# A graph network on one core: overflow one-hots sooner, their products later, 512-byte edge fetches, a third PSUM bank for building

## The chip, the core and the metric

The kernel runs on one core of a Trainium2 chip. The metric is the device time of one execution in microseconds (us), the slowest core's time, which here is the only core's. The engines are named as in the profile: PE is TensorE's matrix product, PEld its weight load, DVE is VectorE, ACT is ScalarE, POOL is GpSimd, SP is SyncE, which issues most plain DMAs. Line numbers (L1108) are those of the kernel before.

## What is computed

There are 6250 nodes with 256 features each and 100000 directed edges, sorted by their destination. The input is normalised per row and passed through ReLU; then come four layers that add to each node the sum over its incoming edges and run a small network of three weight matrices; the input is added at the end.

```python
def agg(h):
    return jax.ops.segment_sum(h[src], dst, num_segments=N)
for l in range(NL - 1):
    h = x + agg(x)
    h = jax.nn.relu(h @ W1s[l] + b1s[l])
    h = jax.nn.relu(h @ W2s[l] + b2s[l])
    x = h @ W3s[l] + b3s[l]
h = x + agg(x)
h = jax.nn.relu(h @ cW1 + cb1)
h = jax.nn.relu(h @ cW2 + cb2)
return h @ cW3 + cb3
...
h = jnp.maximum(_layernorm(x, axis=-1), 0.0)
x = x + _L0_gnn_ref(h, src, dst, ...)
```

## The kernel before

**Two ways to sum over edges.** The nodes lie in 49 blocks of 128. Since the sum over edges is linear, the first matrix of a layer is applied ahead of it: `XY` holds z = x W1, split into a high and a low part that TensorE multiplies without loss. Eight *panels* of up to four blocks are summed by TensorE: for each panel the kernel has a matrix of counts (how many edges lead from node s to node d), and `product` (L1545) multiplies it with XY, tile after tile; the product itself stands at L1566, and `prepare` casts the count tiles from bytes to floats ahead of it (L1539 on ScalarE, L1541 on VectorE) into a short ring of tiles. Twenty-one further blocks (17 in the later layers) are *gathered* by GpSimd: each node has K = 17 slots, each slot one row of z fetched from a table in DRAM by its edge's source (L1391), and VectorE adds the rows up (`pair`, L1417 and L1419, then `fold`, L1429 to L1437).

**Overflow.** A node with over 17 edges has the rest of them put into OV = 2 extra slots that its whole block shares: 256 places for a block. `overflow` (L855) finds for each place its edge and its node: it makes a one-hot `hit` on VectorE (L858), multiplies it on TensorE with `taken` into a PSUM bank of its own, `pt` (L861), turns the result into an edge number and a node number `rel` (L868 to L871), and GpSimd fetches the edge's source with `ask` (L607), 4 bytes for each partition. The rows of these two slots arrive in tiles named `last`. At the end of a block's fold VectorE makes a one-hot `hot` of `rel` (L1439), and `add` multiplies it with the rows into the bank `sums` (L1445); `finish` adds the sums to the fold's result (L1455) and hands it to the small network (L1466, L1260, L1289, L1286).

**Stages.** In the start and the edge search, up to 128 us, the kernel finds where each node's edges begin and computes z. The 21 fetches of the first 17 edges' sources, 68 bytes for each partition, are all asked for at its end (L607, tile `idx`), from the input `src` itself. Then comes the *pre-stage*, 36 ticks of two building steps each, 128 to 185 us. A *building step* (`build`, L1086) makes two pieces of a count matrix: VectorE compares cells with lanes into one-hots `lo` and `hi` (L1067; ScalarE copies the pairs for them at L1062), TensorE multiplies them into a bank `bp` (L1108), and ScalarE (L1116) or VectorE (L1118) copies the counts to bytes; L1121 adds each node's own row. Layer 0 follows, 185 to 840 us: seven panels of 49 units, each unit one step of the product, with the rest of building spread among the units. Layers 1 to 3 take the remaining 1560 us and have no building.

**What sets the order.** It is written out by hand. `tick` counts units; `later(n, f)` runs f n units on; `job` gives a span of units in which the small network may run. A `Gathered` object for each layer spreads its work over a clock of planned TensorE time: `passed` adds an instruction's planned time and sends the row gathers that are due (`flow`), each behind a TensorE instruction (`after`), and `advance` runs the events (pair, fold, add) whose slot has come. A block has SLOT = 19 slots; before the change fold stands at slot 16 and add at slot 18. `begin` starts that clock in the pre-stage, at building step READY = 50 for layer 0, with `slot_rows` (L850), which turns all 21 blocks' fetched sources into rows in two VectorE operations (L852, L853): slots that a node does not use get a row of zeros. Overflow of a block runs two blocks ahead.

**Space in PSUM.** There are eight banks: one for `pt`, one for `sums`, two for the small network, two for `agg` of a panel, two for building.

## Time and profile before

| | us |
|---|---|
| median of 3 runs | 2399.58 |
| lowest and highest run | 2398.6, 2402.63 |
| profiled execution, own time | 2401.84 |
| profiled execution, span from first to last instruction | 2400.0 |

The mean granted TensorE clock of the profiled execution is 0.945 of full speed. A row of the groups reads: line, engine, operation, written tile <- read tiles, shapes, number of instructions | busy us, mean ns of one | idle us of the engine just before them and what ended it. "issue" stands for idle time in which the engine waited for nothing that the profile shows, "remote" for a signal that the profile cannot place. A row of the windows gives, for a stretch of the span, its length and then each engine's busy time with the number of instructions, the granted clock, the share of time in which DMA engines were busy, and the GB/s that they moved. A row of the timeline gives start, duration, engine, line, operation and, in brackets, the idle time before it and what ended it.

### The profile page before, as it was taken

The numbers are of one execution on the slowest core, as the hardware profiler recorded it, in microseconds if no ns is written. First come the engines' busy times: TensorE is split into PE (matmuls) and PEld (weight loads), VectorE is DVE, ScalarE is ACT, GpSimd is POOL, SyncE is SP. The second block draws the span as 40 slices with busy tenths as digits, with TensorE's granted clock in tenths as the row PEclk, the third lists the DMA queues.
The fourth block names the chain that finished last, engine by engine and source line by source line (L and its number), as shares of the span: only waits on it lengthen the run. The fifth ranks groups of instructions, "written<-read, shape, count | busy, mean of one in ns | idle before, by whom it ended". The sixth has DMA issues, their size and how long they took to land.

```text
span 2400.0 us, 28926 instructions
## 1 busy us (share of the span) xinstructions
PE 2107.7 (88%) x9071; PEld 1578.9 (66%) x9071; DVE 1242.1 (52%) x2785; ACT 962.7 (40%) x1925; POOL 1515.7 (63%) x1495
## 2 busy tenths in 40 slices
PE   5858788787888899999999899989998998999898
PEld 3635565555555577777777777767776776676665
DVE  6867665655566634444344544443445444544444
ACT  4756555555455643233223342322323422232222
POOL 3346677666776627776677357776777276777773
PEclk9958999898999999999999999999999999999999
DMA  5425545544454645445455465454546454555553
GB/s 174 133 85 161 167 149 163 163 149 143 147 168 152 210 146 169 145 140 169 138 163 164 151 191 153 138 168 136 171 138 194 150 180 141 175 161 181 162 180 94
DMA packets 198743, 375.68 MB, mean 157 GB/s; under 512 B 34210, under 2 KB 125474, under 8 KB 198580
## 3 DMA queue, kind: packets, MB, share of 16 engines
q0 software_dynamic: 69024, 182.29, 25.8%
q1 hardware_dynamic: 127630, 189.61, 24.4%
q10 hardware_dynamic: 1926, 1.85, 0.3%
q8 instruction: 73, 1.20, 0.2%
q14 instruction: 90, 0.74, 0.1%
HBM read 313.88 MB, written 59.39 MB: 156 GB/s over the span
## 4 chain that ended last, share of the span: by engine, by line
PE 80%; issue 7%; DVE 5%; ACT 3%; another core or an unknown queue 3%; DMA 1%; POOL 0%; ACTq 0%; DVEq 0%; POOLq 0%
PE agg L1566 57%; PE ps L1260 6%; PE ps L1289 5%; PE bp L1108 4%; PE sums L1445 3%; ACT at L1116 1%; PE ps L1286 1%; ACT a L1539 1%; PE bp L953 1%; PE ps L1466 1%; DVE acc L1419 1%; PE ps L582 1%; DVE hi L1067 0%; DVE lo L1067 0%
## 5 line engine op out<-in xcount | busy, mean ns | idle before, releaser
L1566 PE MATMUL agg<-a,XY 128*128 128x512 f32 x6076 | 1584.7, 413 | 58.1 <-issue 34.9
L1391 POOL DMA_INDIRECT rows<-table,idx x1152 | 1179.3, 1024 | 631.0 <-PE agg L1566 245.2
L1566 PEld LDWEIGHTS agg<-a,XY 128*128 128x128 f32 x6076 | 1157.2, 195 | 340.4 <-issue 68.8
L1539 ACT CAST a<-at 128x512 fp32r<-128x512 uint8 x943 | 565.0, 623 | 797.8 <-PE agg L1566 574.2
L1541 DVE CAST a<-at 128x512 fp32r<-128x512 uint8 x576 | 257.1, 452 | 534.7 <-PE agg L1566 368.9
L1116 ACT CAST at<-bp 128x392 uint8<-128x392 f32 x402 | 184.2, 488 | 296.7 <-PE bp L1108 107.3
L1419 DVE TENSOR_TENSOR acc<-acc,rows 128x512 f32<-128x512 f32 x432 | 295.6, 684 | 2.7 <-DMA rows<-table,idx 0.4
L1108 PE MATMUL bp<-hi,lo 128*128 128x196 bf16 x1024 | 158.1, 272 | 119.1 <-issue 68.7
L1108 PEld LDWEIGHTS <-lo 128*128 128x128 bf16 x1024 | 87.3, 104 | 207.6 <-issue 154.8
L1391 POOL DMA_INDIRECT last<-table,over x144 | 154.2, 1071 | 67.4 <-PE agg L1566 27.8
L1260 PE MATMUL ps<-h,w 128*128 128x512 f32 (+2 forms) x364 | 159.3, 578 | 7.0 <-issue 7.0
L1067 DVE TENSOR_TENSOR lo<-lanes,pairs 128x512 bf16<-128x512 bf16 x256 | 107.2, 419 | 73.1 <-remote 32.1
L1067 DVE TENSOR_TENSOR hi<-cols,pairs 128x784 bf16<-128x784 bf16 x256 | 142.8, 558 | 0.0
L1289 PE MATMUL ps<-w,h 128*128 128x256 f32 x588 | 135.9, 383 | 3.5 <-ACT h L1473 1.8
L1289 PEld LDWEIGHTS ps<-w,h 128*128 128x128 f32 x588 | 112.5, 192 | 21.8 <-ACT h L1473 2.6
L1118 DVE CAST at<-bp 128x392 uint8<-128x392 f32 x110 | 62.0, 564 | 121.9 <-PE bp L1108 53.2
L1260 PEld LDWEIGHTS ps<-h,w 128*128 128x128 f32 (+1 forms) x364 | 64.8, 186 | 75.2 <-issue 69.3
L1307 DVE TENSOR_TENSOR zz<-ps,w 128x512 f32<-128x512 f32 (+1 forms) x75 | 49.8, 677 | 122.7 <-PE ps L1289 55.9
L1445 PE MATMUL sums<-last,hot 128*128 128x256 f32 x288 | 81.5, 407 | 35.7 <-DVE hot L1439 20.7
L1455 DVE TENSOR_TENSOR u<-u,sums 128x256 f32<-128x256 f32 x72 | 30.0, 417 | 139.9 <-PE agg L1566 112.7
L1445 PEld LDWEIGHTS sums<-last,hot 128*128 128x128 f32 x288 | 54.9, 198 | 63.3 <-DVE hot L1439 25.3
L1391 POOL DMA_INDIRECT last<-table,idx x72 | 75.0, 1041 | 33.5 <-issue 13.7
(167 smaller groups left out, 1080.8 us busy)
## 6 DMA issues: line engine op xcount, KB each, us to landing
at<-mat SPq DMA_DIRECT2D x214, 448.0 KB
mat<-at SPq DMA_DIRECT2D x32, 784.0 KB
rows<-table,idx POOLq DMA_INDIRECT x1152
table<-zz SPq DMA_DIRECT2D x72, 256.0 KB
back<-table SPq DMA_DIRECT2D x120, 128.0 KB
xs<-in_x_dram SPq DMA_DIRECT2D x8, 768.0 KB
table<-zs SPq DMA_DIRECT2D x24, 256.0 KB
out_dram<-zz SPq DMA_DIRECT2D x24, 256.0 KB
```

The source lines that it names most:

```text
L1067: nc.vector.tensor_tensor(o.rearrange("p q (n t) -> p q n t", t=2), values.rearrange("p (n t) -> p n t", t=2)[:, None, :, :].to_broadcast( ...
L1108: mm = nc.tensor.matmul(bp[:, m * HW:(m + 1) * HW], lo[:, q + m, :], hi[:, q + m, :], start=True, stop=True)
L1116: nc.scalar.copy(o, v)
L1118: nc.vector.tensor_copy(o, v)
L1260: mm = nc.tensor.matmul(ps[:mp, :w], weights[l][0][:, c, i * P:i * P + mp], h1[:, c, :w], start=(c == 0), stop=(c == KC - 1))
L1289: mm = nc.tensor.matmul(o, h2[0][:, c, nodes], w3[:, c, :], start=(c == 0), stop=(c == KC - 1))
L1391: got = nc.gpsimd.indirect_dma_start(out=t, out_offset=None, in_=tables[self.l][:, :], in_offset=bass.IndirectOffsetOnAxis(ap=at, axis=0),)
L1419: nc.vector.tensor_tensor(self.acc, self.acc, t, OP.add)
L1445: mm = nc.tensor.matmul(sums[:, :C], self.hot[:, j, :], self.rows.pop((g, K + j)), start=(j == 0), stop=(j == OV - 1))
L1539: nc.scalar.copy(o, mat[l, p][j])
L1541: nc.vector.tensor_copy(o, mat[l, p][j])
L1566: mm = nc.tensor.matmul(agg[c][:, :w], XY[:, j, o:o + P], a[:, :w], start=(j == 0 and half == 0), stop=(j == NT - 1 and half == 1))
```

## The change

- **One bank for masks and sums.** `sums` is allocated once; its first half takes the overflow products, its second half the mask products that went to `pt`.
- **Building gets a third bank**, from two.
- **Edge fetches 512 bytes wide.** Two DMAs at the start, on ScalarE's queue, copy src into a DRAM tile `srcs`, with 128 elements more at its end. The fetches read 128 elements for each partition from it in place of 17 or 1. The first 17 edges' sources are no longer asked for all at once: `slot_rows` runs once for a block, in each of ticks 1 to 21 of the pre-stage, into a tile from the pool of the row gathers, and five ticks later two small VectorE operations (`turn`) write that block's part of `idx`. An overflow's two fetches go into `run` tiles, of which there are two, and six units later `keep` copies the first element of each to `over`.
- **READY** goes from 50 to 54, that is from tick 25 to tick 27, and with it the two first overflows and the start of the row gathers.
- **Events.** The one-hot `hot` becomes an event of its own (`spots`) at slot 8 of its block, from the end of the fold; `add` moves from slot 18 to slot 21, three slots into the next block, but for the last block. Events are sorted by slot.

```diff
     ps_g = ctx.enter_context(tc.tile_pool(name="ps_g", bufs=1, space=PSUM))
+    sums = ps_g.tile([P, 2 * C], F32, name="sums")
     ps_m = ctx.enter_context(tc.tile_pool(name="ps_m", bufs=2, space=PSUM))
...
     from_i = over[:, 0, :]
+    srcs = dram.tile([E + P], I32, name="srcs")
     taken = const.tile([P, NG, 2], BF16, name="taken")
...
     def look(pool):
+        nc.scalar.dma_start(out=srcs[:E].rearrange("(p e) -> p e", p=P - 28),
+                            in_=src.rearrange("(p e) -> p e", p=P - 28))
+        nc.scalar.dma_start(out=srcs[E:].rearrange("(o e) -> o e", o=1),
+                            in_=src[:P].rearrange("(o e) -> o e", o=1))
         firsts_i = pool.tile([1, EB], I32, name="near_i", bufs=1)
...
         at0 = pool.tile([P, NG], F32, name="at0", bufs=1)
-        nc.vector.tensor_scalar(at0, st, float(E - K), None, op0=OP.min)
+        nc.vector.tensor_scalar(at0, st, float(E), None, op0=OP.min)
         nc.vector.tensor_copy(from_i, at0)
-        for c in range(NG):
-            asks.append((idx[:, c, :], src, from_i[:, c:c + 1]))
-        ask(len(asks))
         nc.vector.memset(taken[:, :, 0], 1.0)
...
 
-    def slot_rows():
-
-        nc.vector.scalar_tensor_tensor(live, idx, pad[:, 1:2], live, op0=OP.add, op1=OP.mult)
-        nc.vector.tensor_scalar(idx, live, pad[:, 0:1], None, op0=OP.add)
+    def slot_rows(gath, c):
+
+        t = gath.tile([P, 2, C], F32, name="rows", bufs=7)[:, 0, :P].bitcast(I32)
+        asks.append((t, srcs, from_i[:, c:c + 1]))
+        ask(1)
+
+        def turn():
+            w = live[:, c, :]
+            nc.vector.scalar_tensor_tensor(w, t[:, :K], pad[:, 1:2], w, op0=OP.add, op1=OP.mult)
+            nc.vector.tensor_scalar(idx[:, c, :], w, pad[:, 0:1], None, op0=OP.add)
+
+        later(5, turn)
 
...
         nc.vector.tensor_scalar(hit, slots, gained[:, c:c + 1], None, op0=OP.is_ge)
-        ps = ps_g.tile([P, W], F32, name="pt")
+        ps = sums[:, C:]
         for j in range(OV):
...
         def gather():
+            ts = [hots.tile([P, P], I32, name="run", bufs=2) for _ in range(OV)]
             for j in range(OV):
-                asks.append((over[:, j, c:c + 1], src, e_i[:, j:j + 1]))
+                asks.append((ts[j], srcs, e_i[:, j:j + 1]))
             ask(OV)
+
+            def keep():
+                for j in range(OV):
+                    nc.vector.tensor_copy(over[:, j, c:c + 1], ts[j][:, 0:1])
+
+            later(6, keep)
 
...
                 self.alone = {b + i for b, n, i, _ in self.blocks}
-                self.rows, self.us, self.acc, self.hot = {}, [], None, None
+                self.rows, self.us, self.acc, self.hot = {}, [], None, {}
                 self.order = [(g, k) for g in range(len(self.blocks)) for k in range(SLOT)]
...
                 for g in range(len(self.blocks)):
+                    behind = 3 if g < len(self.blocks) - 1 else 0
+                    self.events.append((SLOT * g + 8, lambda g=g: self.spots(g), False))
                     for k in range(3, K - 1, 2):
-                        self.events.append((SLOT * g + k, lambda g=g, k=k: self.pair(g, k)))
-                    self.events.append((SLOT * g + K - 1, lambda g=g: self.fold(g)))
-                    self.events.append((SLOT * g + SLOT - 1, lambda g=g: self.add(g)))
+                        self.events.append((SLOT * g + k, lambda g=g, k=k: self.pair(g, k), False))
+                    self.events.append((SLOT * g + K - 1, lambda g=g: self.fold(g), False))
+                    self.events.append((SLOT * g + SLOT - 1 + behind, lambda g=g: self.add(g), True))
+                self.events.sort(key=lambda o: o[0])
                 self.n = len(self.events)
...
             def meets(self):
-                return self.due() and self.events[self.done][0] % SLOT == SLOT - 1
+                return self.due() and self.events[self.done][2]
 
...
                 while self.due():
-                    at, run = self.events[self.done]
+                    at, run, _ = self.events[self.done]
                     self.send(at + 1)
...
                     nc.vector.tensor_tensor(self.acc, self.acc, t, OP.add)
+
+            def spots(self, g):
+                c = self.blocks[g][3]
+                hot = self.hot[g] = work.tile([P, OV, P], F32, name="hot", bufs=2)
+                nc.vector.tensor_tensor(hot, colf[:, None, :].to_broadcast([P, OV, P]),
+                                        rel[:, c, :, None].to_broadcast([P, OV, P]), OP.is_equal)
 
...
                 nc.vector.tensor_tensor(u, u, self.rows.pop((g, K - 1)), OP.add)
-                self.hot = work.tile([P, OV, P], F32, name="hot", bufs=2)
-                nc.vector.tensor_tensor(self.hot, colf[:, None, :].to_broadcast([P, OV, P]),
-                                        rel[:, c, :, None].to_broadcast([P, OV, P]), OP.is_equal)
-
             def add(self, g):
                 b, n, i, _ = self.blocks[g]
+                hot = self.hot.pop(g)
                 for j in range(OV):
-                    mm = nc.tensor.matmul(sums[:, :C], self.hot[:, j, :], self.rows.pop((g, K + j)),
+                    mm = nc.tensor.matmul(sums[:, :C], hot[:, j, :], self.rows.pop((g, K + j)),
                                           start=(j == 0), stop=(j == OV - 1))
...
             (l, p, j) for l in range(NLAYER + 1) for p in range(last[l] + 1) for j in range(NT)]
-        sums = ps_g.tile([P, W], F32, name="sums")
         TAIL = 10.0
...
             name="ps_a", bufs=2, space=PSUM
-        ) as ps_a, tc.tile_pool(name="ps_b", bufs=2, space=PSUM) as ps_b:
+        ) as ps_a, tc.tile_pool(name="ps_b", bufs=3, space=PSUM) as ps_b:
             begun = {0: clock[0]}
-            READY = 50
+            READY = 54
             spread = {u: [] for u in range(2, 2 * PRE + 1, 2)}
...
                 if built[0] == READY:
-                    slot_rows()
                     layers[0].begin()
+                if built[0] % 2 == 0 and built[0] // 2 <= NG:
+                    slot_rows(gath, built[0] // 2 - 1)
                 for c in spread[built[0]]:
```

## Prediction

> **What bounds the kernel now.** I read the page first: busy shares, the chain that ended last, the granted clock.
>
> ```profile
> PE 2107.7 (88%) x9071; PEld 1578.9 (66%) x9071; DVE 1242.1 (52%) x2785; ACT 962.7 (40%) x1925; POOL 1515.7 (63%) x1495
> PE 80%; issue 7%; DVE 5%; ACT 3%; another core or an unknown queue 3%; DMA 1%; POOL 0%; ACTq 0%; DVEq 0%; POOLq 0%
> PEclk9958999898999999999999999999999999999999
> ```
>
> TensorE sets the end: 88% busy, 80% of the chain. The change removes none of its large products, so it can only win back TensorE's idle time, or clock. One slice, the third, has a clock of 0.5. So I cut the span at the stages: start, edge search (45 to 128 us, left out), pre-stage of 36 ticks (128 to 185), layer 0 with building beside it (185 to 840), layers 1 to 3.
>
> ```profile
> core 0: us, PE busy (x) PEld busy (x) DVE busy (x) ACT busy (x) POOL busy (x), PEclk, DMA share, GB/s
> 0.00:45.00 45.00, 20.57 (x66) 13.68 (x67) 31.69 (x80) 19.09 (x39) 12.65 (x35) 0.96 0.57 172
> ...
> 128.00:185.00 57.00, 31.70 (x150) 16.38 (x150) 36.19 (x91) 33.48 (x83) 23.54 (x24) 0.52 0.31 96
> 185.00:840.00 655.00, 539.75 (x2617) 386.70 (x2618) 416.01 (x962) 363.81 (x796) 448.80 (x433) 0.93 0.52 161
> 840.00:2400.00 1560.00, 1448.32 (x5860) 1108.34 (x5859) 695.47 (x1471) 490.38 (x892) 994.93 (x969) 0.96 0.51 158
> ```
>
> TensorE is idle for 25 us of the pre-stage, 115 of layer 0 and 112 of layers 1 to 3. TensorE's groups, stage by stage, say ahead of which line:
>
> ```profile
> L1108 PE MATMUL bp<-hi,lo 128*128 128x196 bf16 x144 | 31.4, 346 | 26.4 <-issue 12.4 <-ACT at L1116 5.3 <-DMA idx<-in_src_dram,over 4.5
> ...
> L1108 PE MATMUL bp<-hi,lo 128*128 128x196 bf16 x880 | 126.7, 260 | 92.7 <-issue 56.3 <-ACT at L1116 21.4 <-DVE at L1118 5.8
> ...
> L861 PE MATMUL pt<-taken,hit 128*128 128x2 bf16 x38 | 4.0, 173 | 10.7 <-DVE hit L858 6.1 <-DVE at L1121 3.3 <-issue 1.2
> ...
> L1566 PE MATMUL agg<-a,XY 128*128 128x512 f32 x4740 | 1185.4, 407 | 51.8 <-issue 32.0 <-DVE a L1541 8.4 <-ACT a L1539 8.2
> ...
> L1445 PE MATMUL sums<-last,hot 128*128 128x256 f32 x206 | 59.3, 413 | 29.8 <-DVE hot L1439 15.0 <-issue 5.5 <-DVE u L1436 5.3
> ```
>
> The first row is the pre-stage, the next two layer 0, the last two layers 1 to 3. In layer 0 the idle time stands ahead of building (92.7 of 115), which has two banks. In the later layers L1445, the overflow product, has 29.8 us ahead of it, mostly ended by the fold's own VectorE operations.
>
> **Start (+1).** Two copies of src into DRAM are new on ScalarE's queue. The chain of the start waits for this fetch among others:
>
> ```profile
> 0.74 6.44 DMA near_i<-in_dst_dram
> ```
>
> 400 KB read and 400 KB written at the 172 GB/s of this stretch are 4.7 us of DMA. Nothing waits for the copy itself before 128 us, so the ends are 0 (other fetches hide it: DMA share 0.57) and +4.7 (all of it ahead of near_i). I take +1, near the first.
>
> **Pre-stage, gathers (-2.1).** Before, 21 edge fetches are issued back to back and run into the first ticks:
>
> ```profile
> 127.09 0.96 POOL L607 DMA_INDIRECT idx<-in_src_dram,over  x1 [0.30 <-issue]
> 128.35 0.96 POOL L607 DMA_INDIRECT idx<-in_src_dram,over  x1 [0.30 <-issue]
> ...
> 130.00:150.00 20.00, 6.42 (x30) 3.17 (x28) 5.87 (x14) 6.26 (x14) 13.67 (x14) 0.51 0.16 40
> 152.00:170.00 18.00, 13.27 (x64) 6.86 (x62) 15.19 (x39) 14.36 (x36) 0.00 (x0) 0.50 0.27 89
> ...
> 139.37 0.48 PE L1108 MATMUL bp<-hi,lo 128*128 128x196 bf16 x2 [1.65 <-issue]
> ...
> 157.09 0.88 PE L1108 MATMUL bp<-hi,lo 128*128 128x196 bf16 x4 [0.18 <-ACT at L1116]
> ```
>
> With GpSimd gathering (14 in 20 us) TensorE does 30 matmuls; without, 64 in 18 us, 0.281 us each. Thirty at that pace are 8.4 us, so 11.6 us are lost, 0.83 for each gather. The row at 139.37 shows how: a pair of matmuls waits 1.65 us where clean pairs wait 0.18, though no engine is the bound. After the change one gather is asked for in each of ticks 1 to 21, with TensorE's last matmul ahead of it, and each is 512 bytes wide. Ends: nothing each (-11.6), or 0.83 each as now (17.4, so +5.8). A lone gather meets one of a tick's two hand-offs, so I take half, 0.45 each: 9.5 against 11.6.
>
> The Trainium skill, "SBUF — State Buffer", section "Who interferes with whom", has GpSimd share ports with VectorE alone: "PE and ACT never wait on anyone." By it a gather would cost TensorE nothing, and this term would be -11.6. The two windows above disagree, since both engines halve their pace, though not by which path.
>
> **Pre-stage, VectorE (+3.8).** Two operations on 357 columns go; 42 on 17 columns come, two a tick, with four small copies for the runs.
>
> ```profile
> L852 DVE SCALAR_TENSOR_TENSOR live<-idx,pad,live 128x357 f32<-128x357 int32 x1 | 0.6, 586 | 0.0
> L853 DVE TENSOR_SCALAR idx<-live,pad 128x357 int32<-128x357 f32 x1 | 0.4, 408 | 0.0
> L868 DVE COPY rel<-pt 128x2 f32<-128x2 f32 x21 | 3.2, 154 | 13.1 <-PE pt L861 7.9 <-issue 3.0 <-PE bp L1108 1.5
> L869 DVE SCALAR_TENSOR_TENSOR e_f<-pt,nodes,line 128x2 f32<-128x2 f32 x21 | 4.4, 208 | 0.0
> L871 DVE TENSOR_SCALAR e_i<-e_f 128x2 int32<-128x2 f32 x21 | 3.9, 184 | 0.7
> ...
> 175.53 0.42 DVE L1067 TENSOR_TENSOR lo<-lanes,pairs 128x512 bf16<-128x512 bf16 x1 [0.16 <-PE bp L1108]
> ```
>
> By L869 and L871 two are 0.39 us; the wide L852 and L853 give 0.99 as the upper end. VectorE has 0.16 us of slack in a clean tick (last row), so 0.23 x 21 = 4.8 stands on the path, less 1.0 for the wide ones. Ends: -1 (the gathers' waits cover all) and 0.83 x 21 - 1 = +16.4.
>
> **Pre-stage, third bank (-1.8).** Clean ticks show 0.18 us of TensorE waiting for ScalarE's copy. A third bank keeps ScalarE fed; I take 0.12 in the 15 ticks without a gather. Ends: 0 and 36 x 0.18 = 6.5.
>
> **Pre-stage, the runs (+2.5).** An overflow's fetches go to `run` tiles, two buffers, freed by `keep`, six ticks after. The second overflow's fetches therefore wait on GpSimd for the first one's keep; layer 0's row gathers are queued behind. Its own keep, on VectorE one tick on, waits for those fetches to land, and the one-hots behind it, so TensorE too. Two gathers at 1.26 us (the rows at 127.09 and 128.35) are 2.5; ends 0 and 4. Pre-stage in all: -2.1 + 3.8 - 1.8 + 2.5 = +2.4.
>
> **Layer 0 (-21).** A third bank lets TensorE run one copy further ahead:
>
> ```profile
> L1116 ACT CAST at<-bp 128x392 uint8<-128x392 f32 x402 | 184.2, 488 | 296.7 <-PE bp L1108 107.3 <-remote 90.0 <-PE agg L1566 51.0
> ```
>
> That is 0.49 us more slack ahead of each of 440 steps. The gaps that a copy ended (21.4 + 5.8 = 27.2) are the bank's own price; I take three quarters, 20. Of the 56.3 "issue", where nothing is seen to be late, I take none, since a long stall empties any number of banks; its end is all of it. L861 keeps its wait for hit, a hot one-hot half a block sooner takes 3 off L1445, and row gathers, begun two ticks later, run 2 us denser: -20 - 3 + 2. Masks now share the sums' bank, so a mask might wait for L1455's read; in the order of instructions no such wait is new, hence 0. Ends 0 and -84. What is late next is ScalarE's cast of the adjacency tile, for the product behind the building step.
>
> **Layers 1 to 3 (-19).** All waits ahead of the overflow product, then one of them in time:
>
> ```profile
> PE sums L1445 <- DVE hot L1439: 15.0, 4, 6.7
> ...
> PE sums L1445 <- issue: 5.5, 1, 5.5
> PE sums L1445 <- DVE u L1436: 5.3, 2, 3.5
> PE sums L1445 <- DVE u L1437: 4.0, 2, 3.2
> ...
> 1679.17 0.42 DVE L1541 CAST a<-at 128x512 fp32r<-128x512 uint8 x1
> 1679.51 0.42 DVE L1429 TENSOR_TENSOR u<-XY 128x256 f32<-128x256 f32 x1
> ...
> 1681.22 0.42 DVE L1439 TENSOR_TENSOR hot<-colf,rel 128x256 f32<-128x256 f32 x1
> ...
> 1681.69 1.65 PE L1445 MATMUL sums<-last,hot 128*128 128x256 f32 x3 [5.50 <-issue]
> ```
>
> Nine gaps. VectorE, held up till 1678, runs the cast of the next tile (done at 1679.59), then the fold and the one-hot (1681.64), and TensorE starts at 1681.69. With the one-hot made half a block earlier and the product three gathers later, TensorE goes on once the cast is there: 2.1 us of the 5.5. What held VectorE up stays. Nine times 2.1 is 19. Ends: 0 (the next tile's cast is as late) and -29.8. The fold has the same length as before, less the one-hot, and finish still follows. Clock 0.96 leaves at most 4% of 1560 us, of which I count none.
>
> **Sum.** +1 + 2.4 - 21 - 19 = -36.6. The profiled execution took 2401.84 us (span 2400.0), the three runs 2398.6 to 2402.63 with median 2399.58; it lies among them, so 2401.84 - 36.6 = **2365 us**.
>
> **Rivals.**
>
> *Narrow fetches are the trouble (2327, chance 0.22).* One rule would make the widening the main gain: narrow fetches disturb what follows.
>
> ```profile
> L607 POOL DMA_INDIRECT idx<-in_src_dram,over x21: 951/955/1322, 120.3 to 146.3; - x21
> ...
> L607 POOL DMA_INDIRECT over<-in_src_dram,e_i x42: 951/957/1301, 171.9 to 762.4; - x42
> ...
> 415.52 0.95 POOL L607 DMA_INDIRECT over<-in_src_dram,e_i  x1 [0.30 <-issue]
> ...
> 425.43 0.87 PE L1108 MATMUL bp<-hi,lo 128*128 128x196 bf16 x4 [7.65 <-issue]
> ```
>
> For it: layer 0's longest gap (7.65 us) opens two microseconds after a 4-byte fetch. Against it: GpSimd's time is the same at 68 and 4 bytes a partition, and the gap at 1676 comes among 1 KB row gathers alone. It would take another 9.5 off the pre-stage and half of the 56.3 "issue": 2365 - 9.5 - 28 = 2327. The Trainium skill, "DMA: Bandwidth & Descriptors", section "Specifications", gives 512 B as the least transfer for line rate, with a read-modify-write below.
>
> *The waits only move (2397, chance 0.11).* TensorE's gaps end with the tile for L1566 in place of a bank or a one-hot. For it: 8.2 and 8.4 us ahead of L1566 end with those casts already. Then the two stages give 8 together, against +3.4: 2397.
>
> *Gathers set the pre-stage's pace (2411, chance 0.15).* If a gather makes its tick as slow as in the window from 130 (7.5 ticks in 20 us, 2.67 each), 21 such ticks, 15 of 1.125 (16 ticks in 18 us) and the wait of 2.5 make 75.5 us where 57 stood: +18.5, and +1 at the start. It ends slower once the later stages give less than 19.5; where late hand-offs, and not buffers, make the gaps, a bank and an earlier one-hot give some 10: 2401.84 + 9.5 = 2411. Against it: each fetch stands alone among a tick's work.
>
> **How the numbers follow.** The forecast (2345 to 2390) gets 0.52. A measurement here can tell 0.2%, that is 2394.8 to 2404.4 for no change. Faster: 0.52 + 0.22 + 0.04 of the moved waits = 0.78; same: 0.07; slower: 0.15. The range, 2325 to 2403, holds the forecast, most of the first rival and the second.
>
> **What would show it.** Right: the pre-stage at 57 to 62 us with matmul pairs waiting under 1 us; the idle time ahead of L1108's line near 70 in layer 0, with a copy's share below 10; ahead of the overflow product under 12 in layers 1 to 3, and L1566's idle time not up by the same. Wrong: a pre-stage over 70 us; "issue" ahead of building below 30 (narrow fetches); L1566's idle time in the later layers over 70 (moved). The most doubtful term is layer 0's.

## The result and the profile after

The changed kernel takes 2416.52 us (median of 6 runs, 2410.72 to 2423.85); the kernel before takes 2401.09 beside it (6 runs, 2391.3 to 2403.4). The ratio is 1.0069, with a 95% interval of 1.0047 to 1.0091: **slower by 0.7%**, some 16 us, where 1.5% faster was forecast. The profiled execution of the changed kernel took 2423.85 us, 22 more than that of before.

The page of the changed kernel, busy times and the granted clock:

```profile
span 2422.0 us, 28894 instructions
...
PE 2120.1 (88%) x9071; PEld 1577.8 (65%) x9071; DVE 1245.0 (51%) x2867; ACT 961.0 (40%) x1925; POOL 1516.9 (63%) x1495
...
PEclk9958998899998999999999999999999999999888
```

TensorE is as busy as before (2107.7 then, the same 9071 products), in a longer span. Where the 22 us lie is read from six instructions that mark the stages, in the timeline of the kernel before: the first building product, the first product of layer 0, and the last activation of each layer's last panel.

```profile
129.79 0.50 PE L1108 MATMUL bp<-hi,lo 128*128 128x196 bf16 x4 [4.51 <-DMA idx<-in_src_dram,over]
...
185.62 2.07 PE L1566 MATMUL agg<-a,XY 128*128 128x512 f32 x4 [0.97 <-ACT a L1539]
...
857.18 0.69 ACT L1582 ACTIVATE h<-agg,bias 128x512 f32<-128x512 f32 x1 [6.34 <-PE agg L1566]
...
1373.06 0.69 ACT L1582 ACTIVATE h<-agg,bias 128x512 f32<-128x512 f32 x1 [1.35 <-PE agg L1566]
...
1881.55 0.69 ACT L1582 ACTIVATE h<-agg,bias 128x512 f32<-128x512 f32 x1 [1.35 <-PE agg L1566]
...
2386.34 0.69 ACT L1582 ACTIVATE h<-agg,bias 128x512 f32<-128x512 f32 x1 [6.98 <-PE agg L1566]
```

The same six in the changed kernel, where L1126 is the building product, L1589 the large product and L1605 the activation:

```profile
132.91 1.62 PE L1126 MATMUL bp<-hi,lo 128*128 128x196 bf16 x8 [3.74 <-DVE hi L1085]
...
188.78 2.07 PE L1589 MATMUL agg<-a,XY 128*128 128x512 f32 x4 [1.03 <-ACT a L1562]
...
868.39 0.69 ACT L1605 ACTIVATE h<-agg,bias 128x512 f32<-128x512 f32 x1 [6.36 <-PE agg L1589]
...
1382.68 0.69 ACT L1605 ACTIVATE h<-agg,bias 128x512 f32<-128x512 f32 x1 [5.21 <-PE agg L1589]
...
1894.13 0.69 ACT L1605 ACTIVATE h<-agg,bias 128x512 f32<-128x512 f32 x1 [5.19 <-PE agg L1589]
...
2402.74 0.69 ACT L1605 ACTIVATE h<-agg,bias 128x512 f32<-128x512 f32 x1 [7.63 <-PE agg L1589]
```

Differences of these starts, the last one to the end of the span (within that tail, 6.2 us before and 11.9 after pass from the end of this activation to the end of TensorE's last product, which is meant by "TensorE's tail" below):

| stage | before, us | after, us | change | forecast |
|---|---|---|---|---|
| start and edge search | 129.8 | 132.9 | +3.1 | +1 |
| pre-stage | 55.8 | 55.9 | 0 | +2.4 |
| layer 0 | 671.6 | 679.6 | +8.0 | -21 |
| layers 1 to 3 | 1529.2 | 1534.4 | +5.2 | -19 |
| tail | 13.7 | 19.3 | +5.6 | 0 |

This is one profile for each kernel, and that of the changed kernel is the slowest of its six executions. In two further profiles of the changed kernel (e5 and e12 below) layer 0 takes 677.2 and 673.1 us, and layers 1 to 3 take 1531.2 and 1533.0: a stage's change is sure to a few microseconds only.

The groups of TensorE in the changed kernel: pre-stage, then layer 0 (three rows), then layers 1 to 3 (two rows).

```profile
L1126 PE MATMUL bp<-hi,lo 128*128 128x196 bf16 x144 | 30.1, 363 | 26.1 <-DVE hi L1085 19.1 <-ACT at L1134 3.2 <-issue 1.9
...
L1126 PE MATMUL bp<-hi,lo 128*128 128x196 bf16 x880 | 126.1, 260 | 106.5 <-issue 59.0 <-ACT at L1134 26.2 <-DVE hi L1085 13.4
...
L872 PE MATMUL sums<-taken,hit 128*128 128x2 bf16 x38 | 3.9, 172 | 9.1 <-issue 6.7 <-DVE hit L869 2.2
...
L1589 PE MATMUL agg<-a,XY 128*128 128x512 f32 x4704 | 1180.1, 406 | 73.9 <-issue 46.2 <-ACT a L1562 19.6 <-DVE a L1564 5.6
...
L1469 PE MATMUL sums<-last,hot 128*128 128x256 f32 x204 | 53.7, 384 | 1.7 <-DMA last<-table,over 1.7
```

Two things are to be seen. In layer 0 the idle time ahead of building is 106.5 us with three banks, where it was 92.7 with two. In layers 1 to 3 the change did what it says, 29.8 us ahead of the overflow product became 1.7, but the idle time ahead of the large product went from 51.8 to 73.9. The wait went to the next product. Taken over the whole of layers 1 to 3, TensorE's idle time is about what it was: 103.6 us before (1529.16 less 1425.59 busy) and 101.3 after (1534.35 less 1433.04).

### The profile page after: what moved, and what is told of

Its sections match the earlier page's. It is cut to its first block, busy times and chain, and to the rows that moved or that the text cites. A ratio compares the mean times of both kernels' runs of the same rounds, so it can differ in the third digit from the quotient of the medians.

```text
span 2422.0 us, 28894 instructions
## 1 busy us (share of the span) xinstructions
PE 2120.1 (88%) x9071; PEld 1577.8 (65%) x9071; DVE 1245.0 (51%) x2867; ACT 961.0 (40%) x1925; POOL 1516.9 (63%) x1495
## 4 chain that ended last, share of the span: by engine, by line
## 5 line engine op out<-in xcount | busy, mean ns | idle before, releaser
L1589 PE MATMUL agg<-a,XY 128*128 128x512 f32 x6076 | 1589.8, 413 | 79.5 <-issue 47.1
L1589 PEld LDWEIGHTS agg<-a,XY 128*128 128x128 f32 x6076 | 1152.6, 195 | 376.7 <-issue 93.9
L1126 PE MATMUL bp<-hi,lo 128*128 128x196 bf16 x1024 | 156.2, 275 | 132.6 <-issue 60.8
L1126 PEld LDWEIGHTS <-lo 128*128 128x128 bf16 x1024 | 83.4, 105 | 218.0 <-issue 130.5
L1278 PE MATMUL ps<-h,w 128*128 128x512 f32 (+2 forms) x364 | 165.3, 595 | 6.1 <-DVE zz L1325 4.5
L1307 PE MATMUL ps<-w,h 128*128 128x256 f32 x588 | 140.9, 391 | 12.1 <-ACT h L1497 10.9
L1307 PEld LDWEIGHTS ps<-w,h 128*128 128x128 f32 x588 | 115.2, 197 | 32.6 <-ACT h L1497 12.7
L1281 ACT ACTIVATE h<-ps,bias 128x512 f32<-128x512 f32 (+2 forms) x91 | 58.9, 663 | 86.5 <-PE ps L1278 42.1
L1469 PE MATMUL sums<-last,hot 128*128 128x256 f32 x288 | 76.6, 387 | 5.6 <-DVE u L1462 3.0
```

Of the source, the lines that this page charges most:

```text
L1126: mm = nc.tensor.matmul(bp[:, m * HW:(m + 1) * HW], lo[:, q + m, :], hi[:, q + m, :], start=True, stop=True)
L1278: mm = nc.tensor.matmul(ps[:mp, :w], weights[l][0][:, c, i * P:i * P + mp], h1[:, c, :w], start=(c == 0), stop=(c == KC - 1))
L1307: mm = nc.tensor.matmul(o, h2[0][:, c, nodes], w3[:, c, :], start=(c == 0), stop=(c == KC - 1))
L1469: mm = nc.tensor.matmul(sums[:, :C], hot[:, j, :], self.rows.pop((g, K + j)), start=(j == 0), stop=(j == OV - 1))
L1589: mm = nc.tensor.matmul(agg[c][:, :w], XY[:, j, o:o + P], a[:, :w], start=(j == 0 and half == 0), stop=(j == NT - 1 and half == 1))
```

## The experiments

There are two sorts of chip. On one chip the kernel before takes 2398 us, close to the 2401 above; on three others it takes 2191 to 2195. These are called the slower and the faster sort below. Each ratio is to the kernel before on the same chip, and only these are compared.

**The parts alone (kernel before in 2193 us).** *e1_bank* takes the masks to the sums' bank and gives building the third bank:

```diff
+    sums = ps_g.tile([P, 2 * C], F32, name="sums")
...
-        ps = ps_g.tile([P, W], F32, name="pt")
+        ps = sums[:, C:]
...
-        ) as ps_a, tc.tile_pool(name="ps_b", bufs=2, space=PSUM) as ps_b:
+        ) as ps_a, tc.tile_pool(name="ps_b", bufs=3, space=PSUM) as ps_b:
```

> The kernel before with one part alone: masks in the second half of the sums' bank, and a third bank for building. Theory A (TensorE's gaps are late hand-offs, which a further buffer does not end, and the loss comes from the start and from the ends of the layers): within 4 us of the kernel before, idle time ahead of the building products 85 to 110 us in layer 0. Theory B (the shared bank itself costs layer 0 its 8 us, by masks waiting for the sums' readers): slower by 6 to 10 us, with the idle time ahead of the mask products well over 10.7 us. The prediction as it stood: faster by 22 us, with 70 us ahead of the building products.

Measured: 2189.03 us, ratio 0.9985 (0.9966 to 1.0003), within theory A's 4 us; B falls. A's second sign failed: the idle time ahead of the building products in layer 0 is 39.3 us, where 85 to 110 were expected. It is 50.8 and 54.6 in e2 and e3, which have two banks, so this sort of chip has smaller gaps to begin with. The third bank took some 11 us of them, and layer 0 was no shorter for it (612.3 us in e1, 610.6 in e2). *e2_events* takes from the change the early one-hot and the later product alone (`spots` at slot 8, `behind = 3`):

> The kernel before with one part alone: the overflow one-hot at slot 8 of its block, the overflow product three slots later. Theory A: the 29.8 us ahead of the overflow product in layers 1 to 3 go, but as much comes ahead of other products, and the later product delays the end of each layer: slower by 3 to 9 us. Theory B (the loss is in layer 0 alone): within 3 us. The prediction as it stood: faster by about 19 us.

Measured: 2205.57 us, ratio 1.0062 (1.0041 to 1.0083), A's sign and more than its 9 us (12.9). *e3_fetch* takes the copy of src, the 512-byte fetches, `keep` and READY alone:

> The kernel before with one part alone: the copy of src, the 512-byte fetches one block a tick, keep, and the later start of the row gathers. Theory A: slower by 3 to 7 us, of which 3 at the start, and the pre-stage within 2 us of before. A rival, that narrow fetches are what disturbs layer 0: faster by over 10 us, with the idle time ahead of the building products in layer 0 under 70 us.

Measured: 2204.29 us, ratio 1.0062 (1.0043 to 1.0081): 11.6 us, above A's 7, since the pre-stage grew by 10 (52.8 us here, 42.8 in e2, both with two banks). The rival's sign, under 70 us ahead of building, is there (54.6), but with the old fetches too (50.8), and the kernel is slower. *e4_soon* is the changed kernel with the product back at slot 18:

```diff
-                    behind = 3 if g < len(self.blocks) - 1 else 0
+                    behind = 0
```

> The changed kernel with the overflow product back at slot 18, all else as changed. Theory A: faster than the changed kernel by 4 to 9 us, which it wins at the ends of the layers and in the tail (from 11.9 us back to about 6 after the last panel). If the place of the product does not matter: within 3 us of the changed kernel, so slower than the kernel before by 12 to 18.

Measured: 2203.3 us, ratio 1.0051 (1.0032 to 1.007). The changed kernel was not timed on a chip of this sort, so e4's two readings are not decided by it; it lies with e3, which has the same fetches. Shared bank and third bank are not the loss; events and fetches are, each by itself. That falls against the rival of narrow fetches: with all fetches wide the kernel is slower. The Trainium skill, "DMA: Bandwidth & Descriptors", section "Specifications", sets 512 B as the least size for line rate. e3 followed it, together with the copy, the ticks and `keep`, and lost 0.6%; what the width alone is worth is not shown, but it did not pay for these.

Why a third bank wins little on this sort of chip shows in what engines wait for in e1's layer 0. First TensorE, then VectorE:

```profile
PE bp L1109 <- DVE hi L1068: 37.7, 31, 3.3
PE sums L1446 <- DVE hot L1440: 16.8, 6, 8.4
PE sums L862 <- DVE hit L859: 13.2, 9, 3.9
```

```profile
DVE acc L1420 <- DMA rows<-table,idx: 81.9, 48, 5.7
...
DVE acc L1418 <- DMA rows<-table,idx: 18.3, 7, 4.9
```

VectorE stands 100 us waiting for gathered rows to land (81.9 + 18.3), and in the kernel's order of its instructions the one-hots of building, of masks and of overflow stand behind those additions. A bank more does not bring a one-hot sooner.

On the slower sort the picture is another. In the first profile, VectorE's longest waits in layer 0 of the kernel before are these, and its list has none for gathered rows:

```profile
DVE at L1118 <- PE bp L1108: 53.2, 41, 5.5
DVE at L1118 <- PE agg L1566: 32.1, 16, 5.5
DVE at L1118 <- remote: 26.6, 8, 6.3
```

TensorE's idle time ahead of building ends with "issue" there for the most part (56.3 of 92.7 us); in e1, 37.7 of 39.3 us end with a one-hot. So what e1 shows may not be carried over to the slower sort.

**What the later product does to the end of a layer.** In e1 (product at slot 18), TensorE near the end of layer 1:

```profile
1230.00 3.59 PE L1261 MATMUL ps<-h,w 128*128 128x512 f32 x8
1233.55 1.48 PE L1446 MATMUL sums<-last,hot 128*128 128x256 f32 x4
```

and the same place in e2 (product three slots later):

```profile
1227.35 3.93 PE L1573 MATMUL agg<-a,XY 128*128 128x512 f32 x16
1234.91 1.19 PE L1452 MATMUL sums<-last,hot 128*128 128x256 f32 x2 [3.63 <-DMA last<-table,over]
1237.20 1.22 PE L1452 MATMUL sums<-last,hot 128*128 128x256 f32 x2 [1.10 <-DMA last<-table,over]
```

The last overflow product of a layer isn't moved. But the one ahead of it is, by five units (by the large products between the two, it stands 18 units ahead of the last in e1 and 13 in e2), and with it the job that hands its group of blocks to the small network. In e1 that network's first product (L1261, 3.59 us) fills the time until the last block's rows land. In e2 it stands behind the last overflow product, and TensorE waits 3.63 and 1.10 us for the rows. In e2's profile layers 1, 2 and 3 are longer than in e1's by 4.9, 4.3 and 2.8 us, and the tail by 3.2.

**The whole on a chip like the first (kernel before in 2398 us).** *e5_after* and, on the same chip in another series, *e12_after2* are the changed kernel itself.

> The changed kernel itself, beside the next three, so that they can be compared with it on one chip, since the chip of the first experiments ran the kernel before in 2193 us. If the parts add up as the first experiments measured them (bank -3.6, events +12.9, fetches +11.6): slower than the kernel before by 18 to 24 us. If the parts' losses overlap: slower by 8 to 16.

> The changed kernel itself, as the measure for the first two on the same chip: slower than the kernel before by 12 to 18 us on a chip like that of the first profile, by 16 to 24 on one like that of the first experiments.

Measured: 2413.23 us, ratio 1.0057 (1.0034 to 1.008), and 2413.48 us, 1.0066 (1.0044 to 1.0088): 15 us by the medians in both, as expected for losses that overlap (8 to 16) and in e12 (12 to 18). The parts as the faster sort measured them do not add up here. *e6_bank_spots* is the kernel before with the shared bank, the third bank and the early one-hot, but `behind = 0` and the old fetches:

> The kernel before with the shared bank, the third bank and the early one-hot; the product stays at slot 18 and the fetches stay as they were. Theory A (the later product and the fetches carry the whole loss): faster than the kernel before by 3 to 10 us. If the early one-hot has a price too: within 2 us or slower.

Measured: 2397.09 us, ratio 0.998 (0.9962 to 0.9998): faster than the changed kernel, and faster than the kernel before by the least that can be told, 5 us by the ratio and 1 by the medians. Which of its two readings holds is not decided. *e7_late* is the kernel before with the later product, the one-hot being an event of its own one slot after the fold:

```diff
+                    self.events.append((SLOT * g + K, lambda g=g: self.spots(g), False))
...
+                    self.events.append((SLOT * g + SLOT - 1 + behind, lambda g=g: self.add(g), True))
```

> The kernel before with the later product alone; the one-hot comes one slot after the fold, as its own event. Theory A (the later product delays the end of each layer and the tail): slower by 8 to 14 us, with the tail after the last panel over 9 us in place of 6. If the early one-hot is what costs: within 3 us of the kernel before.

Measured: 2426.3 us, ratio 1.0104 (1.008 to 1.0128): 28 us by the medians, twice what was expected and more than the whole change. TensorE's tail is 7.9 us, 1.7 over that of before, so the tail is not where most of it lies; by the same marks as above, its one profile has +8 us in layer 0, +2 in layer 1, +8 in layer 2 and +6 in layer 3 with the tail. *e8_apart* is the changed kernel with the first block's overflow six ticks sooner in the schedule:

```diff
-            spread[READY - 4], spread[READY - 2] = [layers[0].blocks[0][3]], [
+            spread[READY - 16], spread[READY - 2] = [layers[0].blocks[0][3]], [
```

> The changed kernel with the first block's overflow six ticks sooner, so that its run tiles are free before the second block asks for them. If the wait for run tiles costs the 6 us that TensorE is idle at the end of the pre-stage: faster than the changed kernel by 4 to 7 us, and that idle time under 1 us. If the row gathers behind it are late anyway: within 2 us of the changed kernel.

Measured: 2412.55 us, ratio 1.0041 (1.0025 to 1.0057). The 6.4 us of idle time at the end of the pre-stage are gone from its profile (pre-stage 49.1 us against 55.4 in e5's); against e5 and e12 the time is better by 0.15 to 0.25%, with intervals that overlap. The ratios do not tell its two readings apart; by the medians e8 is 0.7 us under e5, which is the second. In the profiles layer 0 takes 681.9 us in e8 and 677.2 in e5, so that most of what the pre-stage won is lost again by the end of layer 0. *e9_ends* is the changed kernel with the product at its old slot for the last two blocks of a layer; *e10_bank_ends* is the same with the old fetches:

```diff
-                    behind = 3 if g < len(self.blocks) - 1 else 0
+                    behind = 3 if g < len(self.blocks) - 2 else 0
```

> The changed kernel with the later product for all blocks but the last two of a layer, in place of all but the last. In the changed kernel the second step of the small network of the second-last group stands behind the last block's overflow product, which then waits for its rows. If that is the later product's cost: faster than the changed kernel by 5 to 12 us, won in layers 1 to 3 and the tail (tail near 6 us). If every later product costs a little: within 3 us of the changed kernel.

> The kernel before with the shared bank, the third bank, the early one-hot and the later product but for the last two blocks of a layer; the fetches as before. If the ends of the layers and the fetches are the whole loss: faster than the kernel before by 4 to 10 us, better than with the product at slot 18 (5 us faster). If the later product costs inside the layers too: slower than the kernel with the product at slot 18.

Measured: e9 2406.32 us, ratio 1.0044 (1.0021 to 1.0067); e10 2403.98 us, ratio 1.0023 (1.0006 to 1.0041). By the medians e9 is 7 us under e12, as its first reading has it, with intervals that overlap. TensorE's tail in e9 is 5.2 us in place of 9.5 in e12, and layers 1 to 3 are shorter in its profile (1519.9 against 1533.0), though that execution took 2396.64 us, 10 less than e9's median. Against e6, whose interval does not meet it, e10 says that the later product costs some 0.3 to 0.4% even with the ends put right. Its profile (2399 us, 5 under its median) shows this in layer 0 alone, 677.8 us against 672.1 in e6; layers 1 to 3 are shorter there, 1523.9 against 1529.7.

**No gathers.** *e11_plain_rows* is the kernel before, with a plain DMA of 128 consecutive rows, issued by SyncE, for each row gather. The sums over edges are thereby those of wrong rows; the bytes and the work of the other engines stay.

```diff
-                    got = nc.gpsimd.indirect_dma_start(
-                        out=t, out_offset=None, in_=tables[self.l][:, :],
-                        in_offset=bass.IndirectOffsetOnAxis(ap=at, axis=0),
-                    )
+                    got = nc.sync.dma_start(out=t, in_=tables[self.l][P * (self.sent % 48):P * (self.sent % 48) + P, :])
```

> The kernel before with each row gather of the layers replaced by a plain DMA of 128 rows in a row, issued by SyncE: as many bytes and as many waits, but the wrong rows, and GpSimd idle. If TensorE's gaps in layers 1 to 3 come from GpSimd's gathers (103 us idle, 102 us at half clock on the chip of the first profile): idle time there under 40 us, and the kernel faster by over 60 us. If they come with the DMA traffic or from the order of the work: idle time over 70 us. On a chip such as that of the first experiments, where these gaps are 20 us, the run says little.

Measured: 2113.21 us where the kernel before takes 2398.04, ratio 0.8814 (0.8793 to 0.8835). TensorE is idle for 14.2 us of layers 1 to 3, where it was 103.6: the first reading. Its page, and building in layer 0:

```profile
PE 2010.2 (95%) x9071; PEld 1537.5 (73%) x9071; DVE 1228.8 (58%) x2785; ACT 968.6 (46%) x1925; POOL 109.2 (5%) x127
```

```profile
L1108 PE MATMUL bp<-hi,lo 128*128 128x196 bf16 x880 | 116.6, 251 | 8.6 <-DVE hi L1067 6.4 <-issue 0.7
```

With two banks for building, the idle time ahead of it is 8.6 us, where it was 92.7. The gaps do not come from too few banks. They come with GpSimd's row gathers, and go with them. *e17_plain2* is the same kernel on a chip that runs the kernel before in 2195 us, and beside it and once before, *e18_tiny2* and *e16_tiny* add a 4-byte fetch by GpSimd that nobody uses in each gather's place:

```diff
+                    bits = nc.gpsimd.indirect_dma_start(
+                        out=kth[:, n:n + 1].bitcast(I32), out_offset=None, in_=src.rearrange("(o e) -> o e", o=1),
+                        in_offset=bass.IndirectOffsetOnAxis(ap=at, axis=1),
+                    )
```

> The kernel before with plain DMAs of the wrong rows once more, to see whether the two sorts of chip differ without GpSimd's gathers. If the difference between 2192 and 2400 us comes with the gathers alone: 2110 to 2116 us on a chip that runs the kernel before in 2190 too, as on the one that runs it in 2398. If it is in other work: 2030 to 2100 there.

> The kernel before with plain DMAs of the wrong rows, and besides in each row gather's place a GpSimd fetch of 4 bytes a partition that nobody uses. If a gather disturbs TensorE's hand-offs by being issued (its 128 descriptors and their signals): the gaps come back, 2250 to 2420 us. If it does so by the bytes it moves or by the waits that hang on its rows: within 40 us of 2113.

> Plain rows, and a GpSimd fetch of 4 bytes a partition in each row gather's place, once more. On a chip that runs the kernel before in 2192 this took 2134. On one that runs it in 2398: if the gaps come with issuing a gather, 2250 to 2420; if they come with the bytes or with waits on gathered rows, 2110 to 2150.

Measured: e17 2099.52 us, ratio 0.9572 (0.955 to 0.9594); e16 2133.53, ratio 0.9734 (0.9717 to 0.9751); e18 2134.28, ratio 0.9733 (0.9709 to 0.9757). e17 falls at the upper edge of its second reading (2030 to 2100): the row gathers are not the whole difference. But without them the two sorts of chip are 14 us apart in place of 203, and 10 of the 14 lie in the pre-stage, where 21 edge fetches by GpSimd remain (52.6 us in e11, 42.7 in e17). Nearly all that tells the chips apart comes with GpSimd's gathers. Layer 0 in e17 and in e18, by windows:

```profile
169.00:704.00 535.00, 516.52 (x2680) 375.93 (x2680) 413.87 (x968) 365.33 (x807) 39.43 (x38) 0.99 0.64 198
```

```profile
171.00:736.00 565.00, 523.56 (x2680) 380.33 (x2680) 414.70 (x967) 366.37 (x808) 436.72 (x411) 0.97 0.61 187
```

On the faster sort of chip the issuing of a gather for every row costs layer 0 30 us; with the rows themselves gathered, layer 0 is 613 us (e1, which has a third bank). Issuing is the smaller part there. What is the larger part on the slower sort is not known: e16 and e18 are both of the faster sort, and readings on gaps that this sort hardly has are not decided by them.

**The change without gathers (kernel before in 2191 us, plain rows as in e11).** *e14_bank_spots_plain* is e6, *e15_bank_late_plain* has the shared bank, the third bank and both events as changed, *e13_after_plain* is the changed kernel, each with plain DMAs of wrong rows:

> Shared bank, third bank and early one-hot, with plain DMAs of the wrong rows. With hardly any gaps left in layer 0, a third bank has only the pre-stage to win: 2106 to 2111 us, 2 to 7 under the 2113 of the kernel before so altered. If the bank were worth its 20 us in layer 0 by itself: under 2100.

> Shared bank, third bank, early one-hot and the later product, with plain DMAs of the wrong rows, to be held against the same without the later product. If the later product costs by the order of the small network at the ends of layers: slower by 3 to 8 us. If it cost only by meeting rows that GpSimd has not yet fetched: within 2 us.

> The changed kernel with plain DMAs of the wrong rows in place of the row gathers, to be held against the kernel before so altered, 2113 us. If the change's price is in the order of the work (ends of the layers, ticks of the pre-stage, the wait for run tiles) and does not need the gaps that GpSimd's gathers bring: slower than 2113 by 10 to 20 us. If its price is what the gaps make of it: within 5 us of 2113.

What was expected was held against e11's 2113 us, but on this sort of chip the start is e17's 2099.52. Each ratio is to the kernel before on the same chip (2195 for e17, 2191 for the others, so that by the ratios the first step is -25):

| kernel, plain rows | us | ratio (95%) | step |
|---|---|---|---|
| e17, nothing changed | 2099.52 | 0.9572 (0.955 to 0.9594) | |
| e14, banks and early one-hot | 2072.11 | 0.946 (0.9444 to 0.9476) | -27 |
| e15, and the later product | 2094.48 | 0.9559 (0.9543 to 0.9575) | +22 |
| e13, and the fetches | 2112.82 | 0.9645 (0.9629 to 0.9661) | +18 |

The whole change costs 13 us here (2112.82 - 2099.52; 16 by the ratios), about as much as with the gathers. It has a price without the gaps too, as the first reading of e13 has it, but a price made up otherwise. The later product costs 22, far over the 3 to 8 expected. In the profiles of e14 and e15 it costs nothing in layers 1 and 2 (465.2 and 463.0 us against 465.0 and 463.2), where e2 lost 4.9 and 4.3 with GpSimd's gathers: there the loss seems to come with rows that land late, as the waits of 3.63 and 1.10 us above do. It costs 6.7 us in layer 0 and 18 in layer 3. Of the fetches' 18 us, 13.5 lie ahead of layer 0, which begins at 180.28 us in e13 and at 166.75 in e15. The banks and the early one-hot win 25 to 27 us, far more than the 2 to 7 of e14's first reading; but by the profiles only 10 of it lie in layer 0, where the second has the bank worth 20. Of the rest, 4 are in the pre-stage and 14 in layer 3, where e17 waits ten microseconds ahead of the overflow product:

```profile
PE sums L1442 <- DVE hot L1436: 10.0, 5, 4.2
```

The later product then loses it again, in layer 3 too (437.6 us in e14, 455.8 in e15). TensorE's waits in layer 3 of e15, and VectorE's timeline ahead of the longest:

```profile
PE ps L1261 <- DVE zz L1302: 6.9, 3, 3.1
PE agg L1570 <- DVE a L1545: 4.7, 4, 1.7
PE ps L1471 <- DVE zz L1302: 2.7, 1, 2.7
```

```profile
1796.55 0.69 DVE L1280 TENSOR_TENSOR xt<-xt,cb3r 128x512 f32<-128x512 f32 x1 [5.73 <-DMA xt<-in_x_dram]
...
1798.06 0.69 DVE L1280 TENSOR_TENSOR xt<-xt,cb3r 128x512 f32<-128x512 f32 x1 [0.81 <-DMA xt<-in_x_dram]
...
1799.27 0.42 DVE L1436 TENSOR_TENSOR u<-XY 128x256 f32<-128x256 f32 x1
...
1801.32 1.28 DVE L1302 TENSOR_TENSOR zz<-ps,xt 128x512 f32<-128x512 f32 x2
```

In the last layer the network's third step asks for rows of x and adds them on VectorE at once, which waits for them, 5.73 us here. The next step of the network needs the bank that the result zz frees. In e14 the waits for zz are 1.6 us in all (1.2 + 0.4); with the jobs moved by the later product, the next step comes close behind, and they are 9.6. That is 8 of the 18 us; where the other 10 lie is not shown.

## Why the prediction was wrong, point by point

**Start: right in kind, larger.** +3.1 against +1, within the ends given. In e3, on the faster chip, the first building product comes at 129.6 us, in e2, without the copy, at 129.3; on the slower sort it comes at 129.8 to 132.2 us in the kernels without the copy (before and e10) and at 131.2 to 135.9 with it (e9 and e8). So how much of the 3.1 is the copy stays open.

**Pre-stage: the sum right (0 against +2.4), its terms mixed.** The ticks, by TensorE and by VectorE in the changed kernel, and its end:

```profile
144.20 0.84 PE L1126 MATMUL bp<-hi,lo 128*128 128x196 bf16 x4 [0.42 <-DVE hi L1085]
145.46 0.83 PE L1126 MATMUL bp<-hi,lo 128*128 128x196 bf16 x4 [0.42 <-ACT at L1134]
...
186.80 0.83 PE L1126 MATMUL bp<-hi,lo 128*128 128x196 bf16 x4 [6.40 <-DVE hi L1085]
```

```profile
142.81 0.23 DVE L861 SCALAR_TENSOR_TENSOR live<-rows,pad,live 128x17 f32<-128x17 int32 x1
143.07 0.23 DVE L862 TENSOR_SCALAR idx<-live,pad 128x17 int32<-128x17 f32 x1
...
183.91 0.15 DVE L892 COPY over<-run 128x1 int32<-128x1 int32 x1 [4.41 <-DMA run<-srcs,e_i]
185.70 0.15 DVE L892 COPY over<-run 128x1 int32<-128x1 int32 x1 [1.64 <-DMA run<-srcs,e_i]
```

The two small operations take 0.46 us (0.39 was taken), and a typical tick 1.26 (145.46 - 144.20) where 1.06 was clean: +0.20, as forecast (+0.23). Some ticks wait longer, up to 3.04 us, so that the first 20 take 1.39 us each. The wait for run tiles was found with its mechanism, but mis-sized: 6.40 us against 2.5, since after the two gathers the fetched sources must land as well (4.41 and 1.64 at VectorE); the upper end of 4 was too low. The third bank was worth more than the 1.8 taken: with the old fetches the pre-stage is 49.0 and 50.5 us with three banks (e6 and e10), 55.8 and 53.1 with two (before and e7). So the sum is near because terms offset each other, which is luck. A gather's price of 0.83 us isn't seen when gathers come one a tick: the typical tick of 1.26 is what VectorE's operations explain. On the faster chip the gathers back to back cost next to nothing to begin with (36 ticks in 38.6 us in e1, 1.07 each), and there the fetches' part cost 10 us of pre-stage (52.8 us in e3, 42.8 in e2).

**Layer 0: the step that failed.** The prediction said that the gaps a copy ended, 27.2 us, are the bank's own price and that a third bank takes three quarters of it. By ScalarE's copies alone they were 21.4 with two banks, and with three 26.2 in the changed kernel and 19.7 in e6, so hardly any went. ScalarE's copies themselves wait most for building products (107.3 us) and for "remote" (90.0; the L1116 row in the prediction), so a copy that ends a gap can be the last link of a chain and not the first. e11 removes 84 of the 92.7 us with two banks, and e6, with three and its gathers, none (93.4). What stands at the head of the chain goes with GpSimd's row gathers. The profile before had the evidence, and the prediction used it for the pre-stage alone: the windows with and without gathers. The prediction took nothing off for "issue", rightly, but for the reason that a stall empties any number of banks, which holds for the copies' share too.

The same evidence bears on a rule that the prediction weighed. The Trainium skill, "SBUF — State Buffer", section "Who interferes with whom", has PE and ACT wait on nobody. In e11, with 127 instructions left on GpSimd, TensorE is busy 2010.2 of 2110.3 us; before, 2107.7 of 2400.0. Its idle time falls from 292 to 100 us. No run here shows whether that is by ports; but by whatever path, TensorE did wait on what GpSimd's gathers bring with them, and a kernel can't be priced as if it didn't.

**Layers 1 to 3: the mechanism right, the sum wrong.** The waits ahead of the overflow product went (29.8 to 1.7), as forecast. That TensorE would go on from there was the step that failed. The gap moved to the large product (51.8 to 73.9); waits for ScalarE's casts alone rose from 8.2 to 19.6 there. The prediction had a late cast as the end of its range that gives 0, but counted 2.1 us for each gap, and named ScalarE's cast for layer 0 only. The network's product L1307 waits as well, 12.1 us where it waited 3.5 (L1289 before), nearly all for ScalarE's activation. These two rises, 22.1 and 8.6 us, take back the 28.1 that went. This is the rival "the waits only move", which got 0.11. Its price of 2397 left out what the later product does at the ends of layers. "Finish still follows" was said, and no price given for the network's steps that hang on it: 5.6 us in the tail, and some in the layers. With the products of a layer's last two blocks at their old slot, layers 1 to 3 take 1519.9 and 1523.9 us in one profile each (e9, e10), 5 to 9 less than before: at most so much of the -19 is seen. Rows of the kernel before and of the changed one show how the tail grew:

```profile
2388.48 1.93 PE L1260 MATMUL ps<-h,w 128*64 128x512 f32 x4
```

```profile
2404.77 0.62 PE L1278 MATMUL ps<-h,w 128*64 128x128 f32 x4 [1.60 <-DVE zz L1319]
...
2407.05 3.67 PE L1278 MATMUL ps<-h,w 128*64 128x512 f32 x4
```

A wait of 1.60 us for zz is new, and four products that took 1.93 us take 3.67 after it. The granted clock there is 0.50 (windows, 2407 to 2411 us), where it was 1.00 before (2388 to 2391 us).

**The rival that ended slower gave 2411 us**, near the 2416.5, but by a mechanism that did not happen: the pre-stage was to take 75.5 us and took 55.9. The number is no merit of it.

**What stays open.** Why the later product costs 0.3 to 0.4% on the slower sort of chip (e10 against e6), with layer 0 longer than before by 2 to 10 us in the seven profiles that have it; why it costs 28 us by itself there (e7), and only 13 together with the early one-hot on the faster sort (e2); and by which path a gather delays TensorE's hand-offs there: by being issued, by the scattered rows it reads, or by the waits that hang on them.

## What to carry to other kernels

Before pricing a buffer, look for the first link: cut the windows by whether a suspect engine works, and if the same gaps vanish without it, do not count on a buffer or an earlier operation to end them; here the wait went to the next instruction. A product that is moved by a few slots takes with it every job that hangs on it; price the end of each layer and the tail, where nothing is left to fill in. And a replacement of the suspect by something plain, with wrong data if need be, tells more than undoing parts: it showed 285 us where no part moved more than 28.

## What the runs showed of the hardware that was not expected

The same kernel takes 2398 us on one chip and 2195 on another; with plain DMAs for the row gathers it takes 2113.21 and 2099.52. GpSimd's row gathers cost 12% of the time on the one (ratio 0.8814) and 4% on the other (0.9572), though each takes GpSimd 0.95 us on both. Layers 1 and 2 of the kernel before and of e11, by windows:

```profile
858.00:1882.00 1024.00, 959.86 (x3942) 746.99 (x3943) 455.80 (x972) 333.97 (x613) 661.76 (x646) 0.98 0.52 159
```

```profile
718.00:1648.00 930.00, 928.50 (x3944) 736.25 (x3944) 452.49 (x973) 341.31 (x614) 0.00 (x0) 1.00 0.58 175
```

The same products, each on a chip that runs the kernel before in 2398 to 2400 us: TensorE is idle for 64 of 1024 us beside 646 gathers, and for 1.5 of 930 us beside plain DMAs that move more per second (175 against 159 GB/s). So the amount of traffic is not what disturbs it; the order of the rows, which lie one behind the other for the plain DMAs, was changed as well.
